# The rate at which a planner spreads side work over an attention stream: turns left less 160 instead of less 40

## The chip, the cores and the metric

The kernel runs on one core of a Trainium2 chip. The core has five engines with instruction streams of their own: TensorE (PE, matrix products), VectorE (DVE), ScalarE (ACT, exponentials and tanh), GpSimd (POOL) and SyncE (SP, which issues most DMAs here). The metric is device time in microseconds of the whole launch, the median of several runs; lower is better.

## The reference

Input is an image batch of 4 x 64 x 64 x 128 float32, that is 4 batches of 4096 tokens with 128 channels. Two layers follow each other. Cut to what matters:

```python
# layer 0: two 3x3 convolutions, a gate, causal attention with d_qk = 4, d_v = 16
c1 = conv_same(elu(x), W1, b1)
a, b = split(conv_same(c1, W2, b2), 2)
c3 = a * sigmoid(b)
q, k, v = c3 @ Wq + bq, c3 @ Wk + bk, c3 @ Wv + bv
probs = softmax over the tokens strictly before (q k^T / 4)
x = x + c3 + tile(probs @ v, 8) @ W3 + b3
# layer 1: full attention, 16 heads of 8, over 4096 tokens, then two feed-forwards
t = x
y = layernorm(t)
h = y + softmax(q1 k1^T) v1 @ wo          # q1, k1, v1 = y @ wq, y @ wk, y @ wv
t = t + h + (silu(h @ w1) * (h @ w3)) @ w2
y2 = layernorm(t)
t = t + sum over the best 2 of 8 experts of gate * (y2 @ expert_w + expert_b)
```

The 16 heads' attention of layer 1 has 4 x 16 x 4096 x 4096 scores, and an exponential for each. That is the bulk of the work.

## The kernel before, in words

**Tiles and turns.** The tokens of a batch are cut in 8 blocks (`NQ`) of 512 (`QB`), and the 16 heads in 4 groups (`NG1`) of 4. The unit of the attention of layer 1 is a step: 128 keys against 512 queries for 4 heads, which is four score products on PE into two PSUM tiles `s`, two exponentials on ScalarE of 128 x 1024 elements each (`e<-s`), and four value products on PE into `acc` two turns later (`attention_step`, line 908). A segment (line 1338) is the run of steps over all the keys for one group and one block. One of its 32 key tiles is not given to ScalarE: its exponentials are made by a polynomial on VectorE (`Beside`, line 956; tiles `ey`, `em`, `eg`), and its products are fitted in between.

At the end of a segment `acc` is copied to `at` and stored to memory, `d_a<-at` (line 945). Where the segment is of the last group, the block's attention is complete, and what follows for that block is put on a list as a last part (line 948).

**Fillers.** Everything but the attention stream is written as generators that yield between small pieces of work, each piece with the PE time it takes, mostly 0.46 us, or 0 where the piece has no product of its own and only leaves a turn for something to arrive. The list `fillers` holds them in the order in which they are used, with their remaining PE time by the planner's figures (line 1460): 138.5 us for the preparation of a batch (`first_attention`, line 665, which draws the convolutions and the operands of layer 1 along with it) and 18.3 us for a last part (line 1085: output projection, feed-forward, layernorm, experts and the store of the result). `insert` (line 306) takes the next piece of the first filler.

A last part fetches its operands from memory (`fetch`, line 1073); while one is in its expert products, it starts the fetch of the next (line 1079). Between its layernorm and its expert products the tokens and channels are exchanged (`turned_over`, line 334): within the stream by storing to memory (`d_y<-y`, line 1137), reading back in blocks (`blocks<-d_y`, four DMAs) and a VectorE transpose (`y2T<-blocks`); where no stream runs any more (`alone`), by products with the identity and a copy (`y2T<-s`).

**The loop.** One program is written out at build time by the loop of lines 1476 to 1522, a planner that has no clock of the chip but estimates of its own. Each turn of it emits one attention step, and then decides whether a piece is inserted:

```python
rate = (sum(part[1] for part in fillers) + later) / max(1, sum(steps_left) - 40)
credit = min(3.0, credit + rate)
left = ahead + EXPS - SCORES - (VALUES if len(undone) > 2 else 0.0)
...
elif not turn and (waiting or not quiet[0] and empty and credit > 0.0 and (left >= PIECE or credit > 1.5)):
    took = insert()
    credit -= took
```

`rate` is PE time of side work per turn: all that is on the list, and `later`, what will still come onto it (preparations of batches not begun, and last parts that no segment has released, less the very last), over the turns that the four batches have left, less 40. It is used once the operands of the running batch are complete; until then it is 1. `credit` gathers it, up to 3, and pays for pieces. `left` is the PE time that the turn has free, with `EXPS` = 1.81 us for a turn's exponentials, `SCORES` 0.43, `VALUES` 0.987 and `PIECE` 0.446; what remains of it passes on to the next turn as `ahead`, at most 0.18. A piece goes in where there is credit and room, or where credit is over 1.5 without room. At most one piece goes into a turn, a job of `Beside` takes precedence for the place, and the first two turns of a segment take none. Pieces that need only time ("free") take a turn whatever the credit.

When the steps are over (line 1523) the last products are written, `alone` is set, and line 1525 runs what the list still holds, with no attention beside it. All parts left are chained into one generator there: one after the other.

**Order.** Each engine's instructions run in the order in which they were written (`InOrder`, whose line 113 is the source line of every instruction in the profile). The engines wait for each other by semaphores, and a DMA on SyncE's queue waits there for what it reads, with all that was written after it behind it.

Of the kernel before, what the change touches and what calls it, by code (L numbers as in the profile page):

```python
# [125 lines left out]
def fast_path(ctx: ExitStack, tc: tile.TileContext, a: dict, where: dict, out: bass.AP, verdict):  # L126
# [158 lines left out]
    steps_in, undone, fillers = [], [], []  # L285
    bank_held = [False]

    def do_step(step):
        scores, values = step
        undone.append((values, scores()))  # L290

    def finish(leave):
        while len(undone) > leave:
            values, es = undone.pop(0)
            values(es)
# [10 lines left out]
    def insert():  # L306

        while fillers:
            r = advance(fillers[0])
            if r is not None:  # L310
                return r[0]
            fillers.pop(0)
        return 0.0
# [721 lines left out]
    def beside_work(until, beside_pool=True):  # L1035
        while beside_todo and dve_at[0] + beside_todo[0][0] <= until:
            if not beside_pool and max(dve_at[0], turn_at[0] + 0.5) < pool_at[0]:
                break
            beside_todo.pop(0)[1]()
# [326 lines left out]
    steps_left = [sum(s.hi - s.lo - len(s.beside) for s in plan if s.b == b) for b in range(B)]  # L1366
# [109 lines left out]
    while True:  # L1476
        turn_at[0] += EXPS
        if steps_in:
            do_step(steps_in.pop(0))
        else:  # L1480
            step = next(steps, False)
            if step is False:
                break
            waiting = step is None
            if waiting:
                finish(0)
            else:
                do_step(step)
        b = now[0]
        if batches[b].second == NQ and len(batches) == b + 1 and b + 1 < B:  # L1490
            Batch(b + 1)
            begun = 0
            while begun < len(fillers) and (fillers[begun][2] in fetching or fillers[begun][2] is None):
                begun += 1
            fillers.insert(begun, [first_attention(b + 1, batches[b + 1]), PREPARE, None, False])

        rate = 1.0
        if batches[b].second == NQ:
            later = PREPARE * (B - len(batches)) + LAST * (last_parts_left[0] - 1)
            rate = (sum(part[1] for part in fillers) + later) / max(1, sum(steps_left) - 40)  # L1500
        credit = min(3.0, credit + rate)
        left = ahead + EXPS - SCORES - (VALUES if len(undone) > 2 else 0.0)
        free = bool(fillers) and fillers[0][3]
        turn = not quiet[0] and free and not waiting
        if turn:
            took = insert()
            credit -= took
            left -= took
        can = [job for job in jobs if job.can() and (left >= PIECE or job.late())]
        empty = bank_held[0] or bank_at[0] <= turn_at[0] + 0.3 or batches[b].second < NQ  # L1510
        if can and empty and not (quiet[0] or bank_held[0] or steps_in or waiting):
            can[0].piece()
            left -= PIECE
# [3 lines that stand above are left out]
            left -= took  # L1517
        ahead = min(max(left, 0.0), AHEAD)
        finish(2)
        for job in jobs:  # L1520
            job.step()
        beside_work(turn_at[0] + 2.9, any(job.age > 3 * job.units + 4 for job in jobs if job.halves < 2))
# [681 lines left out]
def conv_attn_hybrid_kernel(tc: tile.TileContext, a: dict, where: dict, out: bass.AP):  # L2204
    nc = tc.nc
    with tc.tile_pool(name="verdict", bufs=1) as pool:
        verdict = pool.tile([1, 1], FP, name="verdict")
        fast_path(tc, a, where, out, verdict)

        beyond = nc.values_load(verdict.bitcast(mybir.dt.int32))  # L2210
        with tc.If(beyond > 0x3F800000):
            general_path(tc, a, where, out)
# [30 lines left out]
```

## Time and profile before

| what | us |
|---|---|
| median of 3 runs | 8030.11 (8029.84 to 8031.65) |
| the profiled execution | 8024.68 |
| its span, first to last instruction | 8022.8 |
| ScalarE busy | 7673.7 (96%) |
| PE busy | 7846.5 (98%) |
| VectorE busy | 4813.6 (60%) |
| GpSimd busy | 675.6 (8%) |

PE's busy time is that of pipelined products with modelled ends, so a PE that reads busy isn't one at its peak. All instructions carry line 113, that of the recording helper, so groups are told apart by their tiles: `e<-s` are the exponentials of the stream, `acc<-e,vg` its value products, `s<-qx,f_kx` its score products; products into `m` are pieces within the stream, and the same products into `s` are pieces outside it. The page's 40 slices of some 200 us each (a digit is the busy share in tenths):

```profile
PE   7999999999999999999999999999999999999997
DVE  4333556463667666656567676656566666666666
ACT  1899999999999999999999999999999999999994
```

### The profile page before, as it was taken

How to read it: one execution, taken by the hardware profiler on the slowest of the kernel's cores; microseconds unless marked ns; L12 is line 12 of the kernel's file. 1: busy time of each engine (PE TensorE's matmuls, PEld its weight loads, DVE VectorE, ACT ScalarE, POOL GpSimd, SP SyncE). 2: the span in 40 equal slices, each digit the busy share in tenths (PEclk: the TensorE clock that was granted, in tenths of full speed). 3: DMA queues.
4: the chain of work that ended last, by engine and by line, in shares of the span. 5: the costliest groups of instructions: out<-in, count | busy, mean ns of one | idle time of the engine just before them, and what ended most of it. 6: DMA issues, size and time to landing. Idle time of an engine off the chain costs nothing. (4 is left out here: it accounts for less than half of the span.)

```text
span 8022.8 us, 177192 instructions
## 1 busy us (share of the span) xinstructions
PE 7846.5 (98%) x73321; PEld 2465.8 (31%) x73321; DVE 4813.6 (60%) x9289; ACT 7673.7 (96%) x8459; POOL 675.6 (8%) x592
## 2 busy tenths in 40 slices
PE   7999999999999999999999999999999999999997
PEld 3232223233332232333332232333333333333333
DVE  4333556463667666656567676656566666666666
ACT  1899999999999999999999999999999999999994
POOL 1201211100012111000003111000000000000000
PEclk9999999999999999999999999999999999999998
DMA  2221010111110101011010100111011111111221
GB/s 73 68 69 66 27 57 31 50 41 61 37 31 14 50 26 48 28 44 43 22 43 14 52 27 27 49 45 41 23 34 49 53 50 53 49 53 48 80 72 31
DMA packets 332341, 356.55 MB, mean 44 GB/s; under 512 B 146083, under 2 KB 222339, under 8 KB 331523
## 3 DMA queue, kind: packets, MB, share of 16 engines
q1 hardware_dynamic: 327507, 343.35, 13.8%
q8 instruction: 577, 9.45, 0.5%
q10 hardware_dynamic: 4016, 1.77, 0.1%
q14 instruction: 241, 1.97, 0.1%
HBM read 209.24 MB, written 135.79 MB: 43 GB/s over the span
## 5 line engine op out<-in xcount | busy, mean ns | idle before, releaser
L113 ACT ACTIVATE e<-s 128x1024 f32<-128x1024 f32 (+1 forms) x8256 | 7610.1, 1095 | 96.8 <-PE s L113 90.3
L113 PE MATMUL acc<-e,vg 128*9 128x512 f32 x31872 | 4218.2, 594 | 0.6 <-DVE at L113 0.6
L113 PE MATMUL s<-qx,f_kx 32*128 32x512 f32 (+1 forms) x16512 | 2688.3, 495 | 36.5 <-DMA f_kx<-d_k 19.3
L113 PEld LDWEIGHTS s<-qx,f_kx 32*128 32x128 f32 (+1 forms) x16512 | 1092.3, 181 | 3876.2 <-ACT e L113 3651.1
L113 DVE SCALAR_TENSOR_TENSOR ey<-ey,eg 128x512 f32<-128x512 f32 x1344 | 952.8, 709 | 32.4
L113 PEld LDWEIGHTS acc<-e,vg 128*9 128x9 f32 x31872 | 723.4, 90 | 799.5 <-issue 412.0
L113 DVE COPY at<-acc 128x512 f32<-128x512 f32 x131 | 90.6, 692 | 669.5 <-PE acc L113 666.1
L113 PE MATMUL m<-v,f_wino 128*32 128x256 f32 x5376 | 429.8, 391 | 11.0 <-POOL v L113 7.3
L113 DVE TENSOR_SCALAR ey<-m 128x512 f32<-128x512 f32 x448 | 307.4, 686 | 78.8 <-PE m L113 75.9
L113 DVE SCALAR_TENSOR_TENSOR ey<-ey,em 128x512 f32<-128x512 f32 x448 | 322.5, 720 | 11.9
L113 POOL TENSOR_TENSOR rs<-ve,f_minus_half 128x4 f32<-128x4 f32 x64 | 65.3, 1020 | 3036.9 <-DVE ve L113 3036.9
L113 DVE SCALAR_TENSOR_TENSOR eg<-em,ey 128x512 f32<-128x512 f32 x448 | 312.8, 698 | 10.4
L113 DVE SCALAR_TENSOR_TENSOR ey<-eg 128x512 f32<-128x512 f32 x448 | 311.5, 695 | 0.0
L113 POOL TENSOR_TENSOR v<-r 128x1024 f32<-128x1024 f32 x112 | 219.2, 1963 | 1091.6 <-PE m L113 1091.2
L113 PE MATMUL m<-f_we,y2T 128*32 128x256 f32 x3712 | 296.5, 391 | 0.0
L113 DVE COPY sd<-m 128x512 f32<-128x512 f32 x168 | 116.0, 691 | 298.7 <-PE m L113 297.4
L113 DVE TENSOR_TENSOR by_e<-m,gates 128x512 f32<-128x512 f32 x232 | 159.4, 687 | 166.2 <-PE m L113 163.0
L113 DVE TENSOR_TENSOR t<-m,t 128x512 f32<-128x512 f32 x59 | 40.8, 692 | 331.0 <-PE m L113 331.0
L113 PE MATMUL m<-hT,f_fw 128*32 128x256 f32 (+1 forms) x2640 | 228.5, 391 | 0.3
L113 POOL TENSOR_TENSOR t<-t,h 128x512 f32<-128x512 f32 x32 | 43.6, 1363 | 2130.3 <-DVE h L113 2130.3
L113 DVE TENSOR_SCALAR em<-em 128x512 int32<-128x512 int32 x448 | 197.2, 440 | 11.1
L113 DVE TENSOR_SCALAR em<-ey 128x512 f32<-128x512 f32 x448 | 195.7, 437 | 12.9
(260 smaller groups left out, 4429.2 us busy)
## 6 DMA issues: line engine op xcount, KB each, us to landing
f_kx<-d_k SPq DMA_DIRECT2D x139, 512.0 KB
qx<-d_q SPq DMA_DIRECT2D x152, 256.0 KB
d_q<-two SPq DMA_DIRECT2D x64, 512.0 KB
d_a<-at SPq DMA_DIRECT2D x128, 256.0 KB
vg<-d_v SPq DMA_DIRECT2D x32, 576.0 KB
d_k<-two SPq DMA_DIRECT2D x32, 512.0 KB
d_v<-vc SPq DMA_DIRECT2D x32, 288.0 KB
xe<-in_x_dram SPq DMA_DIRECT2D x32, 256.0 KB
```

Source lines behind the costliest of these rows:

```text
L113: made = op(*args, **kw)
```

## The change

The number of turns taken from those left is 160, and the least divisor is 40, where it was 40 and 1. Nothing else differs.

```diff
         if batches[b].second == NQ:
             later = PREPARE * (B - len(batches)) + LAST * (last_parts_left[0] - 1)
-            rate = (sum(part[1] for part in fillers) + later) / max(1, sum(steps_left) - 40)
+            rate = (sum(part[1] for part in fillers) + later) / max(40, sum(steps_left) - 160)
         credit = min(3.0, credit + rate)
```

## The prediction

> **What bounds the kernel now.** I read the page's 40 slices first. ScalarE is full from the start of the attention stream to near the end, and the last slice falls off, so the run has two parts: a stream, and a tail in which the pieces left over run alone. The table by stretches gives their sizes (columns: stretch, length, then busy us of PE, weight loads, VectorE, ScalarE and GpSimd with instruction counts, granted PE clock, DMA share, GB/s):
>
> ```profile
> 1600.00:2400.00 800.00, 795.92 (x7330) 243.07 (x7326) 451.70 (x876) 798.31 (x882) 41.68 (x35) 1.00 0.14 43
> ...
> 6400.00:7200.00 800.00, 798.66 (x8119) 252.92 (x8115) 516.16 (x1030) 798.67 (x884) 16.02 (x20) 1.00 0.17 50
> ...
> 7800.00:7904.00 104.00, 103.94 (x1089) 32.85 (x1081) 64.65 (x130) 102.81 (x113) 2.43 (x3) 1.00 0.15 43
> 7904.00:8023.00 119.00, 66.94 (x275) 50.39 (x275) 77.60 (x203) 4.47 (x9) 4.84 (x6) 0.74 0.11 31
> ```
>
> ScalarE is busy 99.8% of the stream's stretches and 4% of the last 119 us. PE reads 99% too, but pipelined matmuls fill that figure; which of the two sets the pace is told by ScalarE's groups. First 1600 to 3400 us, where the planner inserts pieces at a measured rate, then 6300 to 7900 us, where it already inserts one wherever a turn permits:
>
> ```profile
> L113 ACT ACTIVATE e<-s 128x1024 f32<-128x1024 f32 (+1 forms) x1940 | 1784.7, 1102 | 8.0 <-PE s L113 6.5 <-ACT e L113 0.4
> L113 ACT ACTIVATE t<-t 128x512 f32<-128x512 f32 x10 | 7.1, 709 | 0.0
> L113 ACT ACTIVATE th<-h 128x512 f32<-128x512 f32 (+1 forms) x9 | 6.3, 698 | 0.0
> L113 ACT ACTIVATE neg<-xe 128x512 f32<-128x512 f32 x8 | 5.5, 686 | 0.0
> L113 ACT ACTIVATE pr<-lg 128x32 f32<-128x32 f32 x3 | 1.5, 506 | 0.0
> ```
>
> ```profile
> L113 ACT ACTIVATE e<-s 128x1024 f32<-128x1024 f32 x1712 | 1585.3, 1087 | 2.0 <-PE s L113 0.7
> L113 ACT ACTIVATE th<-h 128x512 f32<-128x512 f32 (+1 forms) x42 | 28.6, 681 | 0.0
> L113 ACT ACTIVATE pr<-lg 128x32 f32<-128x32 f32 x13 | 5.6, 430 | 0.0
> ```
>
> Take each window less its other activations and idle time: (1800 - 20.4 - 8.0) / 1940 = 0.913 us per exponential, and (1600 - 34.2 - 2.0) / 1712 = 0.913 us. Densest insertion goes at the same pace, with less idle time. So a piece put into a turn costs PE time that is spare; ScalarE sets the stream. The tail, from VectorE's timeline (start, duration, instruction, idle time before it):
>
> ```profile
> 7904.03 0.69 DVE L113 COPY at<-acc 128x512 f32<-128x512 f32 x1 [6.81 <-PE acc L113]
> 7904.68 0.71 DVE L113 STREAM_TRANSPOSE y2T<-blocks 128x512 f32<-128x512 f32 x1
> ...
> 7949.49 0.69 DVE L113 COPY y2T<-s 128x512 f32<-128x512 f32 x1 [0.57 <-PE s L113]
> ...
> 7995.16 0.69 DVE L113 COPY y2T<-s 128x512 f32<-128x512 f32 x1 [0.57 <-PE s L113]
> ...
> 8014.54 0.69 DVE L113 TENSOR_TENSOR t<-s,t 128x512 f32<-128x512 f32 x1
> ```
>
> The copy of `acc` is the stream's last act. The three `y2T` belong to three last parts, those of blocks 5, 6 and 7 of batch 3: the end of one, then two whole ones in a row, 44.81 and 45.67 us apart. They follow each other because line 1525 chains them into one generator. SyncE's queue at the seam:
>
> ```profile
> 7897.25 0.33 SPq L113 DMA_DIRECT2D d_y<-y  x1
> 7899.32 3.49 SPq L113 DMA_DIRECT2D blocks<-d_y  x4
> 7904.75 0.33 SPq L113 DMA_DIRECT2D d_a<-at  x1
> ```
>
> Block 5's transposing trip through memory is issued while the stream still runs, ahead of the store of the last `at`.
>
> **What the Trainium skill says.** "Perfetto Trace Analysis", section Identifying the Most-Contended Engine, says that ScalarE's occupancy is a fair measure and PE's matmul occupancy is not; both read 99% here, and the equal 0.913 us agrees with going by ScalarE. "Trainium Architecture — The Big Picture", section Inside one NeuronCore, says each engine has its own instruction stream and they meet only at semaphores; that is why moved PE and VectorE work can vanish beside ScalarE. "DMA: Bandwidth & Descriptors", section Anatomy of one DMA, says a semaphore wait is made by the issuing sequencer, before dispatch, so what stands behind a waiting DMA waits too. The trace shows 2.07 us from `d_y` to the first `blocks` issue.
>
> **The change, part by part.** It has no instruction of its own; it moves pieces. What it moves follows from the planner's arithmetic (lines 1476 to 1522), which reads no clock and can be worked through turn by turn; the built programs' instruction order agrees.
>
> (a) Rate. The first 288 turns of 4126 have rate 1 in both. At turn 300, 3717 turns are left, 136.1 us of pieces are listed, and 2 x 138.5 + 31 x 18.3 = 844.3 is still to come: 980.4 / 3677 = 0.267 before, / 3557 = 0.276 after. Late it grows apart, but there the supply of permitted turns is the limit: from about turn 3164 before and 2978 after, a last part takes 62 turns in both. All insertions: 3071 before, 3120 after, 18.3 us of PE time more in the stream. The number of turns, of turns waiting for a batch (4) and of VectorE's exponential jobs is unchanged.
>
> (b) Tail. By turn 4094 before has finished block 4 of batch 3, after has finished block 5. So the stream leaves three parts before (26.8 us by the planner's measure, beside the last) and two after (8.5): the rest of block 6, and block 7. One whole part leaves the tail: the mean of its two intervals, (44.81 + 45.67) / 2 = **45.2 us off**.
>
> (c) That part's ScalarE work goes into the stream, where ScalarE has no room: 3 x 0.681 + 0.430 = **2.5 us on**. Its PE and VectorE work lies beside the exponentials: at nothing, by the equal paces. Without that cover its 18.3 us of PE time would be paid.
>
> (d) The seam. The floor of 40 lets the rate sink to 0.21 in the last turns, credit falls under 1.5, and turns 4119 and 4124 insert nothing. The part cut at the end is thus two steps behind: in SyncE's order the `blocks` loads come after `d_a<-at`, which waits for the last copy of `acc`. They can start at 7904.75 + 0.33 = 7905.1 instead of 7899.32, 5.8 us later. Before, their last issue ended at 7902.81 and the transpose ran at 7904.68, so the landing took at most 1.87 us; after: 7905.1 + 3.49 + 1.2 to 1.87 = 7909.8 to 7910.5. Bounds 5.1 to 5.8, perhaps 1 more where the store shares the DMA engines; I take **5.6 us on**. Nothing hides it: the tail's first work needs `y2T`.
>
> (e) Stalls. In 800 to 7900 us ScalarE lacks 7100 - 7069.3 = 30.7 us, in scattered waits of up to about 4 us where a segment's end meets an unfinished exponential job, or convolutions meet their operands. Shifting pieces re-deals them. Bounds: -30.7 (all gone) and +30.7 (doubled). Densely filled turns show fewer, so I see no drift: **0**, with 10 either way as likely.
>
> (f) Batch 3's preparation now starts behind block 0 of batch 1 and ends at turn 2778 instead of 2751; it is needed at 3134. The other two end 10 and 18 turns earlier. Hidden, at nothing.
>
> Sum: -45.2 + 2.5 + 5.6 = -37.1 us. The profiled execution spans 8022.8 (8024.68 with what lies around it), so the changed span should be 7985.7. The median of the runs, 8030.11, stands 5.4 above the profiled execution; the same step down gives 7993.0.
>
> **Rivals.**
> - Stalls eat the gain. Early pieces are convolution pieces, which wait for GpSimd and VectorE, and those are where the stalls are. For: 2 to 4 us stalls exist. Against: all of them are 30.7 us and the early rate rises by only 3 to 7%. If they doubled: 8030.1 - 37.1 + 30.7 = 8024, no change.
> - The change does nothing: were the last 1000 turns filled before and the backlog the same, the tail would keep three parts: 8030. The 186 turns by which saturation comes sooner, and the order of instructions, speak against it.
> - Slower: PE becomes the pace where pieces are denser. Locally it does: 20 exponentials took 18.62 us at 7884, 0.931 each, beside pieces of the second feed-forward product. If that 0.018 us held for all exponentials between turns 288 and 2978, 5380 of them, it would add 97 us: 8030 - 37 + 97 = 8090. It decides from 53 / 5380 = 0.010 us each. Against: the mean is 0.913 in both windows.
>
> **How the numbers follow.** Forecast 0.92, stalls eating it 0.04, nothing changed 0.01, slower 0.03. The likeliest case gives 7993. Its ends: stalls -10 with the store's bound, 7982; stalls +14 and the DMA one slower, 8008. The other cases hold less than 2 in 10, so the range is 7982 to 8008. About 0.2% (16 us, under 8014) is what can be told from no change: faster 0.92, same 0.05, slower 0.03.
>
> **What would show it.** Right: one `y2T<-blocks` at the seam and one `y2T<-s` after it, 45 us apart; the 118.8 us from the last copy of `acc` to the end shrinking to about 79; `blocks<-d_y` issued after `d_a<-at`; that copy near 7906.5; 3 more tanh in the stream. Wrong: two `y2T<-s` left, the copy beyond 7920, or idle time of ScalarE well over 31 us in the stream.

## The result, and the profile after

| | before | changed |
|---|---|---|
| median, us | 8029.98 (8027.02 to 8031.65, 4 runs) | 7988.12 (7986.05 to 7990.82, 4 runs) |
| profiled execution, us | 8024.68 | 7990.82 |
| its span, us | 8022.8 | 7989.0 |

The ratio is 0.9949, with a 95% interval of 0.9937 to 0.9961: 41.9 us faster, where 37.1 were forecast. The profiled spans differ by 33.8 only; why is said below. First the table by stretches of the changed kernel, cut at its own last copy of `acc` (columns as before: stretch, length, busy us of PE, weight loads, VectorE, ScalarE, GpSimd, PE clock, DMA share, GB/s):

```profile
1600.00:2400.00 800.00, 794.45 (x7324) 241.88 (x7316) 449.52 (x875) 795.36 (x878) 47.46 (x40) 1.00 0.13 41
6400.00:7200.00 800.00, 799.77 (x8100) 253.34 (x8096) 515.17 (x1022) 799.40 (x885) 15.86 (x19) 1.00 0.17 51
7800.00:7909.00 109.00, 108.93 (x1130) 34.70 (x1126) 69.04 (x140) 107.79 (x120) 2.43 (x3) 1.00 0.12 39
7909.00:7989.00 80.00, 42.38 (x163) 31.60 (x163) 48.21 (x129) 2.35 (x5) 2.41 (x3) 0.70 0.11 31
```

ScalarE is as full in the stream as before to within 3 us in 800, and the tail is 80 us long instead of 119. The tail holds 5 ScalarE instructions where there were 9: three tanh and one small exponential fewer, the ScalarE work of one last part. VectorE's timeline of the changed kernel shows which:

```profile
7909.01 0.69 DVE L113 COPY at<-acc 128x512 f32<-128x512 f32 x1 [5.04 <-PE acc L113]
7914.62 0.71 DVE L113 STREAM_TRANSPOSE y2T<-blocks 128x512 f32<-128x512 f32 x1 [4.92 <-DMA blocks<-d_y]
...
7961.45 0.69 DVE L113 COPY y2T<-s 128x512 f32<-128x512 f32 x1 [0.57 <-PE s L113]
...
7980.81 0.69 DVE L113 TENSOR_TENSOR t<-s,t 128x512 f32<-128x512 f32 x1
```

Of the three `y2T` one `y2T<-blocks` and one `y2T<-s` are left. The first now waits 4.92 us for a DMA, which it did not before. SyncE's queue at the seam shows the DMA's place:

```profile
7904.00 0.33 SPq L113 DMA_DIRECT2D d_y<-y  x1
7909.73 0.32 SPq L113 DMA_DIRECT2D d_a<-at  x1
7910.10 2.71 SPq L113 DMA_DIRECT2D blocks<-d_y  x4
```

The four loads now stand behind the store of the last `at`, and begin 6.1 us after the store that they read from was issued; before, that was 2.07 us.

**Where the 33.8 us of the spans come from.** Taken from the starts of these rows and those before:

| piece of the run | before | changed | difference |
|---|---|---|---|
| start to last copy of `acc` | 7904.03 | 7909.01 | +4.98 |
| copy to first `y2T` | 0.65 | 5.61 | +4.96 |
| first to last `y2T` | 90.48 | 46.83 | -43.65 |
| last `y2T` to the last sum into `t` | 19.38 | 19.36 | -0.02 |
| from there to the end of the span | 8.26 | 8.19 | -0.07 |

The sum is -33.80. Of the first row, 4.06 us were there before the programs differ. PE's instructions are the same up to the 298th attention step. The copy of `acc` that belongs to the 288th step, the last end of a segment ahead of that, stands in VectorE's timelines of before and of the changed kernel as

```profile
818.61 0.69 DVE L113 TENSOR_TENSOR at<-acc,part 128x512 f32<-128x512 f32 x1 [2.46 <-PE acc L113]
```

```profile
822.67 0.69 DVE L113 TENSOR_TENSOR at<-acc,part 128x512 f32<-128x512 f32 x1 [2.46 <-PE acc L113]
```

This is one execution against another, not the change: the late-only version below, which is the program of before up to the last batch, has this copy at 822.36 in its trace. The profiled execution of before was 5.3 us under the median of its runs, that of the changed kernel 2.7 over its own; together they make up the 8 us between the difference of the medians and that of the spans.

### The profile page after: what moved, and what is told of

Its sections match the earlier page's. It is cut to its first block, busy times and chain, and to the rows that moved or that the text cites. A ratio compares the mean times of both kernels' runs of the same rounds, so it can differ in the third digit from the quotient of the medians.

```text
span 7989.0 us, 177746 instructions
## 1 busy us (share of the span) xinstructions
PE 7828.8 (98%) x73597; PEld 2454.2 (31%) x73597; DVE 4806.6 (60%) x9289; ACT 7674.3 (96%) x8459; POOL 670.1 (8%) x592
## 4 chain that ended last, share of the span: by engine, by line
PE 90%; issue 4%; DVE 3%; ACT 1%; DMA 1%; POOL 0%; SPq 0%; ACTq 0%; DVEq 0%; POOLq 0%
PE acc L113 44%; PE s L113 28%; PE m L113 19%; DVE ey L113 1%; ACT e L113 1%; DVE t L113 0%; DVE h L113 0%; DMA f_kx<-d_k 0%; DVE at L113 0%; DVE pos L113 0%; DVE em L113 0%; SPq L113 0%; DVE by_e L113 0%; POOL rs L113 0%; DVE eg L113 0%
## 5 line engine op out<-in xcount | busy, mean ns | idle before, releaser
L113 ACT ACTIVATE e<-s 128x1024 f32<-128x1024 f32 x8256 | 7612.7, 1098 | 98.3 <-PE s L113 91.3
```

The source lines that it names most:

```text
L113: made = op(*args, **kw)
```

## The experiments

Every version keeps all of the computation, and all but the last differ in the line of the rate alone. `W` stands for the numerator, `L` for `sum(steps_left)`.

**Which turns carry the gain.** Two complementary halves.

```diff
-            rate = W / max(1, L - 40)
+            rate = W / (max(40, L - 160) if b == B - 1 else max(1, L - 40))
```

> The new divisor in the last batch alone, the old one in batches 0 to 2. By the planner's arithmetic the stream then inserts 3071 pieces, as before, and leaves the same three parts. Tail theory (the gain is one whole part fewer behind the stream): as before, 8030, within 5 us. Rival, that the higher rate itself gains where it rises most (0.82 against 0.47 some 300 turns from the end): most of the gain stays, 7988 to 8000.

Measured: 8028.14 us (8025.68 to 8030.85), ratio to before 0.9999 (0.999 to 1.0007). Three `y2T` stand behind the stream as before, the copy to the first 0.61 us apart. With the backlog of before, the higher rate buys nothing in the last batch: the planner already puts a piece wherever a turn permits, and a rate above that is only a number.

```diff
-            rate = W / max(1, L - 40)
+            rate = W / (max(1, L - 40) if b == B - 1 else max(40, L - 160))
```

> The complement: the new divisor in batches 0 to 2, the old one in the last batch. The stream now ends just after block 6's part has begun (one piece of it is in), so behind the stream stand block 6 nearly whole and block 7. Tail theory: the 20 us from a part's y2T to the next part's first product go from the tail of before, nothing is waited for at the seam: 8030 - 20 + 0.5 = 8010, within 6 us. Rival, that spreading the early pieces otherwise is what gains (stalls of ScalarE taken away): 7988.

Measured: 8004.37 us (8001.52 to 8015.96), ratio 0.9972 (0.9961 to 0.9983): 25.5 us faster, near the tail theory's 19.5 and far from all of the gain. In its trace the tail is 96.2 us long, from the last copy of `acc` at 7911.94 to the end at 8008.1, where it was 118.8 before. The change works through the backlog: pieces done sooner in batches 0 to 2, 18.3 us of them by the planner's measure, leave the last batch with less to do. How much of it shows depends on where the end of the stream cuts a part, which here is at its start.

The two halves do not add up to the 41.9 us of the whole. With the smaller backlog the old divisor no longer fills the last batch: by the planner's measure 283.8 us of pieces go in there, against 293.1 before, with the late-only version and with the change. The traces agree. From 6200 to 7800 us PE has 138 instructions fewer in this version (second row) than in the changed kernel (first row):

```profile
6200.00:7800.00 1600.00, 1599.56 (x16207) 506.25 (x16200) 1017.70 (x2025) 1598.80 (x1768) 34.01 (x42) 1.00 0.18 56
6200.00:7800.00 1600.00, 1598.28 (x16069) 501.89 (x16061) 1010.19 (x2007) 1598.39 (x1767) 33.08 (x40) 1.00 0.18 56
```

So the new divisor is needed in the last batch too, once the early batches have it.

**The seam.**

```diff
-            rate = W / max(40, L - 160)
+            rate = W / max(1, L - 160)
```

> 160 with the old floor of 1: the same two parts are left, cut at the same piece, but no turn at the end goes without a piece, so the blocks loads stand ahead of the last d_a store on SyncE's queue. Seam theory: y2T follows the last copy of acc by 0.7 us instead of 5.6, and the time is 5 us under the changed kernel's, 7983. Rival, that the transposing trip takes so long by itself: y2T still 5 us behind the copy, 7988.

Measured: 7986.05 us (7980.95 to 7990.61), ratio 0.9946 (0.9929 to 0.9962). VectorE's timeline and SyncE's queue of this version:

```profile
7910.85 0.69 DVE L113 COPY at<-acc 128x512 f32<-128x512 f32 x1 [6.82 <-PE acc L113]
7911.46 0.70 DVE L113 STREAM_TRANSPOSE y2T<-blocks 128x512 f32<-128x512 f32 x1
```

```profile
7904.06 0.33 SPq L113 DMA_DIRECT2D d_y<-y  x1
7906.08 2.93 SPq L113 DMA_DIRECT2D blocks<-d_y  x4
7911.57 0.33 SPq L113 DMA_DIRECT2D d_a<-at  x1
```

`d_y` is issued at the same time as in the changed kernel, within 0.1 us, but the loads follow it at once, and `y2T` comes 0.61 us after the copy instead of 5.61. So the place in SyncE's queue made the 5 us, not the trip itself. The medians show 2 of the 5 us, with ranges that overlap: in total the gain of this step isn't resolved; in the trace it is.

**Denser still.**

```diff
-            rate = W / max(40, L - 160)
+            rate = 3.0
```

> A rate of 3 in every turn once a batch's operands are complete: a piece wherever a turn permits one, and nothing is left at the end but block 7's part, which can't begin before the last store. Tail theory: from the last copy of acc, 3.1 us to the store's landing, 9.1 us from the first fetch to an, 54 us from an to the end, 66 us in place of the changed kernel's 80; 7988 - 13.5 + 0.5 = 7975 if ScalarE's stalls stay near 30 us. Rival, PE becomes the pace where pieces are dense (0.931 us per exponential instead of 0.913): up to 97 us more in the stream, 8030 to 8070.

Measured: 7993.31 us (7992.28 to 7995.1), ratio 0.9956 (0.9939 to 0.9973). Both theories missed. The tail is as computed, 65.9 us from the last copy of `acc` to the end of the span, but the copy comes at 7924.60, 15.6 us later than with the changed kernel. ScalarE's groups say what it is made of (first row the changed kernel, second this version, whole span: busy us, mean ns, then idle time before them and its causes):

```profile
L113 ACT ACTIVATE e<-s 128x1024 f32<-128x1024 f32 x8256 | 7612.7, 1098 | 98.3 <-PE s L113 91.3 <-ACT e L113 1.4 <-issue 0.9
```

```profile
L113 ACT ACTIVATE e<-s 128x1024 f32<-128x1024 f32 x8256 | 7619.8, 1093 | 106.0 <-PE s L113 97.2 <-ACT e L113 1.5 <-issue 0.9
```

The same exponentials take 7.1 us more and wait 7.7 us more for their scores. In the first stretch where convolution pieces come densely, before and this version compare so:

```profile
800.00:1400.00 600.00, 595.48 (x5434) 178.86 (x5426) 342.99 (x609) 598.22 (x656) 102.74 (x80) 1.00 0.12 38
```

```profile
800.00:1400.00 600.00, 590.80 (x5608) 179.18 (x5608) 359.12 (x660) 589.52 (x645) 109.91 (x89) 0.99 0.13 43
```

ScalarE lacks 10.5 us instead of 1.8 there and gets 645 instructions done instead of 656. From 6200 to 7800 us, dense in both with the pieces of last parts, ScalarE is idle for 1.6 us in this version and 1.2 with the changed kernel. The loss lies ahead of that, in batches 0 to 2. The copy of `acc` that ends the first segment of the last batch comes 19 us later than with the changed kernel (first row), and all later copies are 15.6 to 19.5 us later:

```profile
6114.07 0.69 DVE L113 COPY at<-acc 128x512 f32<-128x512 f32 x1 [5.23 <-PE acc L113]
6133.14 0.69 DVE L113 COPY at<-acc 128x512 f32<-128x512 f32 x1 [5.24 <-PE acc L113]
```

Only in batches 0 to 2 do the pieces of preparations go in. Whether it is their kind that costs, or how close together they stand, is not shown. The next run tests whether the loss comes with the number of pieces that the stream takes over.

**A little denser.**

```diff
-            rate = W / max(40, L - 160)
+            rate = W / max(1, L - 240)
```

> 240 turns less, floor 1: the early rates lie 2 to 4% over those of 160, and block 6's part just ends within the stream, so block 7's alone is left, as with the densest insertion. If the densest version lost its gain to dense convolution pieces in batches 0 to 2, the last copy of acc comes at 7909 as with the changed kernel, 65.9 us follow as measured there, and the time is 7977, within 5 us. Rival, that the stream pays for each piece it takes over, whatever its kind: the copy comes 10 to 20 us later, 7987 to 7993.

Measured: 7974.75 us (7971.59 to 7978.43), ratio to before 0.9935 (0.9918 to 0.9952), the best of all: 53.5 us under the before of its own comparison (8028.27). VectorE's timeline:

```profile
7904.43 0.69 DVE L113 COPY at<-acc 128x512 f32<-128x512 f32 x1 [3.82 <-PE acc L113]
7915.96 0.69 DVE L113 TENSOR_TENSOR an<-an,per 128x512 f32<-128x512 f32 x1 [6.09 <-DMA per<-d_r]
7936.53 0.69 DVE L113 TENSOR_TENSOR t<-s,t 128x512 f32<-128x512 f32 x1 [3.85 <-PE s L113]
7941.97 0.69 DVE L113 COPY y2T<-s 128x512 f32<-128x512 f32 x1 [0.57 <-PE s L113]
```

One part is left, and 65.3 us lie from the copy to the end at 7969.7. The stream took over more pieces than with the changed kernel (3147 against 3120) and did not get longer; in 800 to 7900 us ScalarE lacks 25.6 us, against 29.1 with the changed kernel and 37.5 with the densest version. By the planner's measure this version and the densest put the same 1063.2 us of pieces into the stream. What cost the densest version its gain is thus the rate in batches 0 to 2, not the number of pieces. The new wait at `an`, 6.09 us, is the price of the last part alone: nothing covers its fetch any more.

**Is the tail a chain?** On the version with the floor of 1:

```diff
-    run_alone([(r for part in fillers for r in part[0])], lambda: False)
+    run_alone([part[0] for part in fillers], lambda: False)
```

> As the version with the floor of 1, but the two parts left behind the stream are written alternately, a piece of each in turn, not chained. If the tail is a chain of latencies in which the engines idle, block 7's an comes about 12 us after the last copy of acc instead of 20.6, and the time falls by some 8 us, 7978. If the tail is bound by VectorE's or PE's work, or the parts block each other's buffers, it stays at 7986 or rises.

Measured: 7981.31 us (7979.6 to 7987.1), ratio 0.9941 (0.9924 to 0.9957); the medians fall by 5 (by 3 where each is taken against its own before, 8028.27 here and 8029.84 for the floor of 1), within ranges that overlap. In the trace, block 7's `an` comes 13.0 us after the copy instead of 20.6, as expected, but 31.3 us instead of 26.5 lie between it and its `y2T`. From the copy to the end it is 71.8 against 74.4 us. So 2.6 of the 7.5 us are kept: the chain can be begun sooner, and the two parts then hinder each other. The trace points to VectorE's queue: from 7931.2 to 7948.1 us, while block 7's feed-forward runs, VectorE is busy for 15.95 of 16.9 us, because block 6's sums (`by_e`) stand between its steps, and the second and third tanh wait 4.58 us each for VectorE, where they waited 2.35 and 2.14. That buffers add to it is not excluded.

## Why the prediction was right, point by point

- (a) The rate moves pieces and nothing else. The halves of the change agree: the new divisor gives nothing in the last batch alone and 25.5 of the 41.9 us in the early batches alone. The rest comes only with both.
- (b) One part leaves the tail. Forecast 45.2 us, measured 43.65. The interval that remains is 46.83 us, longer than both of before (44.81 and 45.67). Most of the excess lies between `an` and `y2T`: 26.6 us, against 24.8 and 25.7. There the sum into `t` waits 4.79 us for PE's second feed-forward product, where it waited 2.66 and 3.57. The stretches with the last 20 instructions of this product, two of before and then the one of the changed kernel, show why (columns as above):

```profile
7941.40:7944.00 2.60, 2.50 (x20) 2.31 (x20) 0.00 (x0) 0.00 (x0) 0.00 (x0) 1.00 0.00 0
7986.20:7989.70 3.50, 3.41 (x20) 3.12 (x20) 0.00 (x0) 0.00 (x0) 0.00 (x0) 0.70 0.00 0
7951.20:7956.00 4.80, 4.63 (x20) 4.34 (x20) 0.02 (x1) 0.00 (x0) 0.00 (x0) 0.50 0.00 0
```

  The same 20 instructions took 2.50, 3.41 and 4.63 us, at a granted clock of 1.00, 0.70 and 0.50. The page "TensorE: Matmul & The Clock Gate" of the Trainium skill (section What's actually happening) says that the clock follows recent activity over a free-running window. That parts with the same work met different clocks fits it, but what set the clock in each is not shown by a run here.
- (c) 2.5 us of ScalarE work into the stream. Not resolved: from the 288th step to the last copy of `acc`, the profiled executions differ from before's by -1.0 us (late only, with as many pieces in the stream as before), -0.2 (240 less), +0.9 (the change), +3.4 and +5.1 (the floor of 1 and the version with alternating parts, whose stream is the change's up to its last turns). The scatter is as large as the term.
- (d) The seam. Forecast 5.6 us, measured 4.96 in the trace. The mechanism stands by the version with the floor of 1. The term was large by 0.6 because the four issues took 2.71 us, not 3.49.
- (e) Stalls. Forecast no net change, measured 29.1 against 30.7 us of missing ScalarE time between 800 and 7900 us. The two versions with nearly the same stream lack 31.5 and 33.1, so the sum moved by less than such executions differ.
- (f) The later end of batch 3's preparation cost nothing that shows: turns that wait for a batch stayed at 4.

Of the rivals, the one with PE as the pace is not borne out. The densest version's stream is 15.6 us longer, not 97, and in its dense stretch from 800 to 1400 us PE is busy less than before (590.80 against 595.48 us). What happens there is nearer to the rival of stalls: ScalarE waits 10.3 us for scores in five waits of up to 4.2 us. The 7.1 us by which the exponentials' busy time grew in that version are not explained.

The 4.8 us by which the medians beat the forecast aren't explained by a term, and they aren't resolved: the interval of the ratio holds 31 to 51 us. The trace alone gives 33.8, or 37.9 without what was there before the programs differ, against the 37.1 of the sum. The two terms that a trace can show, (b) and (d), make up -38.7 us. That (c) and (e) did not move the total further is in part luck, since the length of the stream scatters by some 5 us.

## What to carry to other kernels

Side work hidden beside a saturated engine costs its time only where the cover ends, so count what is left over when the main stream stops; there a part of 18 us of PE time was 45 us of latency. A rate that is already above what the slots accept does nothing when raised, but it has to be worked out again when the backlog has changed. The rate in the early slots decides the backlog, and too dense there it cost 19 us. After any such shift look at the in-order queue at the seam: two turns without a piece put a load behind a store that waits for the last result.

## What was not expected of the hardware

Executions of one program differ by some 4 us at the start: at the copy of `acc` after the 272nd step, ahead of the first instruction of PE in which these three differ (behind the 278th step), they stood at 789.28 us (before), 793.34 (the change) and 789.93 (240 less). The late-only version, the same program as before up to the last batch, stood at 793.02. A span read from one profiled execution each is thus not good for differences under about 5 us, while intervals within a trace, such as copy to `y2T`, repeat: 0.61, 0.61 and 0.60 us in three versions, and 0.65 before.
